# The edge tokens of a neighbour attention move into the first query block, and background work enters between score passes

## Chip, cores and metric

The kernel runs on one core of a Trainium2 chip. The metric is the device time of one execution in microseconds (us). In the text PE is the matrix engine, DVE the vector engine, ACT the scalar engine, POOL the GpSimd engine and SP the engine whose queue issues nearly all DMAs.

## What is computed

Four transformer layers act on one sequence of 2048 tokens with 128 features, all in float32. Each is an attention and a feed-forward part (FFN), both pre-normed and added to the residual `x`:

```
x = x + L0_attn(ln(x)); x = x + L0_ffn(ln(x))   # 16 heads of 8, softmax over all tokens; GELU
x = x + L1_attn(ln(x)); x = x + L1_ffn(ln(x))   # 16 heads of 64, softmax over all 2048 tokens; SiLU gate
x = x + L2_attn(ln(x)); x = x + L2_ffn(ln(x))   # token s sees s-1, s, s+1 (mod 2048); one of 8 experts
x = x + L3_attn(ln(x)); x = x + L3_ffn(ln(x))   # a memory updated in 32 chunks of 64 tokens; 2 of 8 experts + shared
```

Two facts set what may run when. In `L2_attn` each token needs the keys and values of its two neighbours, so a block of 256 tokens needs one token from the block before and one from the block after, and the first token's neighbour is token 2047. In `L3_attn` a state is handed from one chunk of 64 tokens to the next, so the 32 chunks run one after the other.

## The kernel before

**Three parts.** First layer 0 runs with everything it needs. Then the attention of layer 1 runs as a hand-written loop (`l1_attn`, from L1066), the "attention" part below. What follows it for tokens that are ready (layer 1's FFN and all of layers 2 and 3) runs as *background* beside that loop. What background is left when the loop ends is drained in the "tail".

**The attention loop.** `QB` (L33) cuts the 2048 query tokens into five blocks, as (first token, tokens, width). A *unit* is one block and one pair of heads `p`; there are 40 units, eight for each block, and `units` lists them in order. Within a unit the loop of L1136 makes 16 key steps of 128 keys. A step makes four score passes for each of the two heads (the high part of the query `qh` with the high and low parts of the keys `ka`, the low part `ql`, and `mbt` x `onr`, which subtracts a row's maximum), an exp on ACT into `P`, sums of `P` on POOL (`acg`) and DVE (`acd`), and the product of the step before with the values (`P`, `ka`). Between them stand products `km` x `qh` for the maxima of later units, which DVE reduces (`mx`). When a block's eight units are done, `stage_wo` (L1023) applies the output matrix, two pairs at a time, transposes the sum `wac` and adds it to the residual `xs`.

**Edge tokens.** So that layer 2 need not wait for all five blocks, the block (512, 384, 388) carries four more columns: tokens `ex` = 1280, 1792 and 2047, and one of zeros. `u_loadx` (L379) loads them one DMA each; their queries go to `qx`, their maxima through `qx` products of 8 rows (L439). When this block is done, `stage_wo` loads the residual rows of these tokens as `xm` and adds the attention's result. `stage_m` (L1314) carries this small matrix through layer 1's FFN and writes the keys and values of the edges into `edge`. `s_b` (L1959), which starts layer 2's attention of a 256-token block, waits for this `m` and for the blocks that hold neighbours which `ex` does not list.

**Background and order.** The program's order on PE, DVE, ACT and POOL is that in which this Python code emits instructions. Every background stage is a generator, cut into pieces at each `yield`. A `yield 1` asks for a free PSUM bank before the next piece; a `yield "T"` says that the next piece has PE products. `note` (L96) keeps an estimated clock per engine from costs written in L90. `Part.may` (L202) lets a piece in when, by these clocks, its inputs are there and DVE and ACT aren't too far behind. `fill` (L246) takes the first piece that may enter, in the order of `T["order"]`: chunks (`h`), output stages (`d`), then layer 2 and so on, the expert lanes last. With `only="t"` it takes pieces without products alone. The attention loop calls `fill()` twice in each step, after the exps and after the value products. `drain` (L262) empties everything at the end.

**Background stages**, for block `b` of 256 or half-block of 128 tokens: `stage_a` is layer 1's FFN (products `xt` x `wi`), `stage_a2` makes queries, keys and values of layer 2 (`w2m`), `stage_b` its attention (`hb` x `bd8`), `stage_b2` its FFN (`xb`, ending with `oT`); `stage_c` the gates and scans of layer 3's attention, `chunk` (L1626) one state step (`xst` is the new state, `u`, `dz`, `af`, `at` its operands), `stage_d` its output; `stage_g` the router (`rT`), `stage_e0` opens a PSUM bank for the experts of a block, and `s_lane` (L1880) runs the 13 expert tiles of a block, 104 in all, in two lanes and, in the tail, five more. `s_g` lets the router of a block go once the experts of the block before are opened.

Of the kernel before, what the change touches and what calls it, by code (L numbers as in the profile page):

```python
# [14 lines left out]
ALU = mybir.AluOpType  # L15
# [15 lines left out]
ATANH = (1.0000000039388743, 0.3333315796754013, 0.20012426861749952, 0.13980709417165652, 0.14087328632693624)  # L31
T = dict(lead0=22, more0=4, mgap=0.4, pvq=2, lim0=0.5, fq=(3,), pl=-0.5, pr=1.0, tlow=2, tback=3, late=0.3, pvp="mx", mxp="mx", ex=(1280, 1792, 2047), low=1, lows='ge', keep=1, leave=2, pvn=1, sp=0, rdy=40., eu=2, qg=(22, 16, 10), em=2, el=6, sem=0.2, same=1.2, tsame=3.0, order="hdmBbAaEcCeg", ps=dict(st=3, mx=5), dma=2.3, slack=0.1, lim=0.3, backlog=2.5, lead=(10, 8, 6), pp=7, dve=(14, 15), qp=(1, 1), lanes=2, xl=5,
         QB=[(0, 512, 512), (512, 384, 388), (896, 512, 512), (1408, 384, 384), (1792, 256, 256)])  # L33

# [36 lines left out]
def body(ctx: ExitStack, tc: tile.TileContext, x, pa, pb, pc, pi, pd, pr, pr0, pe, pw, out):  # L71
# [122 lines left out]
    class Part:  # L194
# [24 lines left out]
        def step(self):  # L219
            piece[0] = clk["T"]  # L220
            r = next(self.gen, "end")
            self.same = r == "same"
            self.ready = 0.0 if self.same else piece[0] + (r if type(r) is float else 0.0)
            self.pe = r == "T"
            self.banks = r if type(r) is int else 0
            self.seen = len(emitted) if r is False else -1
            if r == "end":
                emitted.add(self.key)
            return r != "end"
# [139 lines left out]
    xnd = dram.tile([128, S], F32, name="xnd")  # L369

    QB = T["QB"]
    EXTRA = T['ex']
    units = [(qb, p) for qb in range(len(QB)) for p in range(NP1)]
    qhh, qfs, kmx, mx1 = {}, {}, {}, {}

    qx = [mid.tile([128, 8], F32R, name=f"qx{i}") for i in range(2)]
    xq = {}

    def u_loadx(qb):  # L379
        t0, tn, n = QB[qb]  # L380
        xq[qb] = l1x.tile([128, 512], F32, name="xq", tag="xq", bufs=2)
        if n != tn:
            ge.memset(xq[qb][:, tn:n], 0.0)
            for i, t in enumerate(EXTRA):
                sy.dma_start(xq[qb][:, tn + i:tn + i + 1], xnd[:, t:t + 1])
        sy.dma_start(xq[qb][:, :tn], xnd[:, t0:t0 + tn])

    def u_qprep(u):
        qb, p = units[u]
        if qb not in xq:  # L390
            u_loadx(qb)
        n = QB[qb][2]
        yield 1
        ps = mi()
        mm(ps[:, :n], C("wq", p * 128, 128), xq[qb][:, :n])
        yield
        qf = l1x.tile([128, 512], F32, name="qf", tag="qf")
        se.activation(qf[:, :n], ps[:, :n], AF.Identity, bias=bq8[:, p:p + 1], scale=0.125)
        rel(ps)
        yield  # L400
        qhh[u] = l1q.tile([128, 512], F32R, name="qh", tag="qh")
        se.copy(qhh[u][:, :n], qf[:, :n])
        yield
        qfs[u] = qf
        tn, n = QB[qb][1:]
        if n > tn:
            for e in range(2):
                r = slice(64 * e, 64 * e + 64)
                se.copy(qx[u % 2][r, 4 * e:4 * e + n - tn], qf[r, tn:n])

# [14 lines left out]
    def u_max(u, i):  # L425

        qb, p = units[u]
        tn, n = QB[qb][1:]
        per = nmax(u) // 4
        c, r = divmod(i, per)  # L430
        qt, e = divmod(r, 2)
        if i == 0:
            mx1[u] = sm.tile([128, 2, 4, 4], F32, name="mx1", tag="mx1")
        if 128 * qt == tn:
            ps = amx()
            mm(ps[0:8], qx[u % 2], kmx[(u, c)])
            ve.tensor_reduce(mx1[u][0:8, 0, 3, c:c + 1], ps[0:8], AX.X, ALU.max)
            rel(ps)
            return 1  # L439
        pss = [amx() for _ in range(2)]  # L440
        for e in range(2):
            rows = slice(64 * e, 64 * e + 64)
            mm(pss[e], qhh[u][rows, qt * 128:(qt + 1) * 128], kmx[(u, c)][rows, :], par=e and 0.02)
        for e in range(2):
            ve.tensor_reduce(mx1[u][:, e, qt, c:c + 1], pss[e], AX.X, ALU.max)
            rel(pss[e])
        return 2

    def u_maxend(u):
# [6 lines left out]
        if n > tn:  # L456
            ve.tensor_reduce(m[0:8, 0, 3:4], mx[0:8, 0, 3, :], AX.X, ALU.max)
        yield 1
        t = mi()
        if n > tn:  # L460
            te.transpose(t[0:1, 256:264], m[0:8, 0, 3:4], ident[0:8, 0:8])
        for e in range(2):
# [4 lines left out]
        if n > tn:  # L467
            for e in range(2):
                se.mul(mbt[u % 2][64 * e:64 * e + 1, tn:n], t[0:1, 256 + 4 * e:256 + 4 * e + n - tn], -1.0)
        rel(t)  # L470
# [552 lines left out]
    def stage_wo(qb, part):  # L1023
# [29 lines left out]
        if n != tn:  # L1053
            ne = len(EXTRA)
            xm = edge_x[0] = sm.tile([ne, 128], F32, name="xm", tag="xm", bufs=1)
            for i, t in enumerate(EXTRA):
                sy.dma_start(xm[i:i + 1, :], xs[t % 128:t % 128 + 1, t // 128, :])
            yield 1
# [7 lines left out]
    def l1_attn():  # L1066
        LEAD = dict(zip((256, 384, 512), T["lead"]))
        LEAD.update({260: LEAD[384], 388: LEAD[512]})
        U = len(units)
# [66 lines left out]
        for g in range(16 * U):  # L1136
# [6 lines left out]
            if u + 2 < U:  # L1143
                if k == 1 and units[u + 2][1] == 0:
                    need(("q", u + 1))
                    u_loadx(units[u + 2][0])
                if k == T["qp"][n <= 256] and u + 2 >= EU:
                    helper(("q", u + 2), u_qprep(u + 2))
# [165 lines left out]
    def stage_m():  # L1314
# [21 lines left out]

        xt = sm.tile([128, 4], F32, name="xtm", tag="xtm", bufs=2)
        yield from norm_T(xt)
        h = sm.tile([128, 12], F32, name="hm", tag="hm", bufs=1)
        for k in range(3):  # L1340
# [3 lines left out]
            yield  # L1344
            th = sm.tile([128, 4], F32, name="thm", tag="thm", bufs=2)
# [3 lines left out]
            ve.scalar_tensor_tensor(h[:, 4 * k:4 * k + ne], th[:, :ne], 0.5, ps[:, 64:64 + ne], ALU.mult, ALU.mult)  # L1349
            rel(ps)  # L1350
            yield 1
        ps = mi()
        for k in range(3):
            mm(ps[:ne, :128], h[:, 4 * k:4 * k + ne], tok(wi, 6 + k), start=(k == 0), stop=(k == 2))
        yield
        ve.tensor_tensor(xm, xm, ps[:ne, :128], ALU.add)
        rel(ps)
        yield
        xt = sm.tile([128, 4], F32, name="xtm", tag="xtm", bufs=2)
        yield from norm_T(xt)  # L1360
        ps = mi()
        for i in range(2):
            mm(ps[:, 4 * i:4 * i + ne], tok(w2m, i), xt[:, :ne])
        yield
        for i in range(2):
            for j, t in enumerate(EXTRA):
                se.activation(edge[:, t // BN, i, int(t % BN > 0):int(t % BN > 0) + 1], ps[:, 4 * i + j:4 * i + j + 1],
                              AF.Identity, bias=b2m[:, i:i + 1])
# [257 lines left out]
    def chunk(b, c):  # L1626
# [48 lines left out]
        ve.scalar_tensor_tensor(u, tht, 2.0, u, ALU.mult, ALU.add)  # L1675
        yield
        mm(da, ef, w2)
# [440 lines left out]
```

## Time and profile before

| what | us |
|---|---|
| median of three runs | 3001.57 (2998.61 to 3004.23) |
| the profiled execution | 3001.08 |
| its span in the profile | 2999.2 |
| PE / DVE / ACT / POOL busy in the span | 2769.9 / 2194.9 / 1582.9 / 1522.3 |
| mean granted PE clock | 0.936 |

The profile's times count from the start of the span. Nearly all instructions are recorded under line L147, since a helper emits them; so groups are told apart by the names of the tiles that they write and read (`mi` is any PSUM bank). A row such as `mi<-km,qh` is a product into PSUM from `km` and `qh`. Matrix products of float32 data show two records each, those of the rounded float32r data one.

### The profile page before, as it was taken

Reading aid. Unit: us, or ns where it says so; the run is one execution under the profiler, and the core shown is the slowest. Engines: PE = TensorE matmul, PEld = TensorE weight load, DVE = VectorE, ACT = ScalarE, POOL = GpSimd, SP = SyncE. Lnnn points to the kernel's source line nnn. Section 1 sums busy time; section 2 is a strip of 40 time slices with the busy share of each in tenths; the row PEclk is TensorE's granted clock in tenths of the full one; section 3 lists DMA queues with packets and bytes.
Section 4 is the critical chain, followed back from the end, with each engine's and each line's share of the span. In section 5 each row is a group of like instructions: output and inputs, shape, how many; then the busy total and the mean of one; then the engine's idle time right before and its main releaser. Section 6 shows DMA issues by size and latency. Waiting matters only on the chain.

```text
span 2999.2 us, 49776 instructions
## 1 busy us (share of the span) xinstructions
PE 2769.9 (92%) x16719; PEld 1307.0 (44%) x16719; DVE 2194.9 (73%) x4699; ACT 1582.9 (53%) x3933; POOL 1522.3 (51%) x1762
## 2 busy tenths in 40 slices
PE   7999999999979899999999999899989898888998
PEld 2222222322234344454444444455544555565666
DVE  7899898898534666566666778887677769787765
ACT  1788887888854444444444444444434334333444
POOL 2400110201127688866776876677767556443444
PEclk9999999999979999999999999999999999776779
DMA  6311231321144333433442332233334343312244
GB/s 142 72 28 22 72 84 17 101 54 46 53 141 135 92 112 110 121 110 111 138 119 87 94 95 87 89 105 108 109 97 114 108 117 94 88 52 61 76 104 115
DMA packets 247749, 275.80 MB, mean 92 GB/s; under 512 B 95747, under 2 KB 183330, under 8 KB 247366
## 3 DMA queue, kind: packets, MB, share of 16 engines
q1 hardware_dynamic: 246630, 272.43, 33.2%
q8 instruction: 132, 2.16, 0.3%
q14 instruction: 123, 1.01, 0.1%
q10 hardware_dynamic: 864, 0.20, 0.0%
HBM read 229.97 MB, written 42.28 MB: 91 GB/s over the span
## 4 chain that ended last, share of the span: by engine, by line
PE 70%; DVE 18%; ACT 6%; issue 3%; DMA 3%; POOL 1%; SPq 0%; ACTq 0%; DVEq 0%; POOLq 0%
PE mi L147 70%; DVE mx L147 5%; ACT P L147 3%; DVE sB L147 1%; DVE o L147 1%; DVE gq L147 1%; DMA ka<-kvd 1%; DVE gt L147 1%; DVE xs L147 1%; ACT kf L147 1%; ACT kh L147 1%; DVE xn L147 1%; DVE sG L147 1%; DVE acd L147 1%; DVE sA L147 0%
## 5 line engine op out<-in xcount | busy, mean ns | idle before, releaser
L147 DVE TENSOR_REDUCE mx<-mi 128x1 f32<-128x512 f32 (+1 forms) x2080 | 1322.1, 683 | 582.8 <-PE mi L147 571.5
L147 ACT ACTIVATE P<-mi 128x512 f32<-128x512 f32 (+3 forms) x2304 | 1137.0, 551 | 1004.1 <-PE mi L147 973.2
L147 POOL TENSOR_TENSOR acg<-acg,P 128x512 f32<-128x512 f32 (+3 forms) x960 | 1011.4, 1083 | 181.8 <-ACT P L147 180.0
L147 PE MATMUL mi<-P,ka 128*64 128x512 f32 (+3 forms) x2560 | 597.6, 546 | 2.3 <-DVE mx L147 2.3
L147 PE MATMUL mi<-qh,ka 64*128 64x512 f32 (+3 forms) x2560 | 521.0, 406 | 9.7 <-DMA ka<-kvd 6.8
L147 PEld LDWEIGHTS mi<-qh,ka 64*128 64x128 f32 x2560 | 247.0, 189 | 382.5 <-issue 347.0
L147 PE MATMUL mi<-kop,qop 48*128 48x512 bf16 x1024 | 348.6, 405 | 24.5 <-DVE mx L147 12.1
L147 PE MATMUL mi<-qop,kop 50*128 50x512 bf16 x1024 | 317.8, 391 | 27.1 <-ACT P L147 24.7
L147 PE MATMUL mi<-P,vop 128*32 128x512 f32 x2048 | 304.3, 623 | 13.9 <-ACT P L147 13.9
L147 POOL TENSOR_SCALAR vep<-mv 128x2 f32<-128x2 f32 (+1 forms) x24 | 5.5, 229 | 495.6 <-DVE mv L147 495.6
L147 PE MATMUL mi<-km,qh 64*128 64x512 f32 x1024 | 225.6, 410 | 30.4 <-DVE mx L147 23.8
L147 PE MATMUL mi<-mbt,onr 64*128 64x512 f32 (+3 forms) x1280 | 228.7, 351 | 1.5 <-DMA mbt<-mb 1.5
L147 PE MATMUL mi<-ql,ka 64*128 64x512 f32 (+3 forms) x1280 | 229.2, 353 | 0.0
L147 PEld LDWEIGHTS mi<-P,ka 128*64 128x64 f32 x2560 | 129.2, 137 | 225.3 <-issue 195.1
L147 PEld LDWEIGHTS <-kop 50*128 50x128 bf16 x1024 | 63.6, 95 | 304.9 <-issue 281.6
L147 POOL TENSOR_TENSOR acg<-P 128x512 f32<-128x512 f32 (+3 forms) x80 | 91.1, 1158 | 202.5 <-DVE acd L147 162.0
L147 PEld LDWEIGHTS mi<-km,qh 64*128 64x128 f32 x1024 | 107.1, 189 | 60.5 <-DVE mx L147 38.5
L147 PEld LDWEIGHTS mi<-mbt,onr 64*128 64x128 f32 x1280 | 124.6, 190 | 13.9 <-DMA mbt<-mb 2.2
L147 PEld LDWEIGHTS mi<-ql,ka 64*128 64x128 f32 x1280 | 125.7, 192 | 0.0
L147 PEld LDWEIGHTS <-qop 48*128 48x128 bf16 x1024 | 72.9, 96 | 97.2 <-issue 82.7
L147 PEld LDWEIGHTS mi<-P,vop 128*32 128x32 f32 x2048 | 55.5, 109 | 119.8 <-issue 90.7
L147 POOL TENSOR_TENSOR kl<-kf,kh 128x512 f32<-128x512 f32 x32 | 40.9, 1278 | 110.9 <-ACT kh L147 82.4
(509 smaller groups left out, 3464.4 us busy)
## 6 DMA issues: line engine op xcount, KB each, us to landing
ka<-kvd SPq DMA_DIRECT2D x320, 384.0 KB
km<-khd SPq DMA_DIRECT2D x159, 256.0 KB
khd<-kh SPq DMA_DIRECT2D x32, 256.0 KB
kvd<-kh SPq DMA_DIRECT2D x32, 256.0 KB
kvd<-kl SPq DMA_DIRECT2D x32, 256.0 KB
kvd<-vt SPq DMA_DIRECT2D x16, 512.0 KB
ka<-in_pw_dram SPq DMA_DIRECT2D x37, 192.0 KB
w3s<-in_pw_dram SPq DMA_DIRECT2D x35, 192.0 KB
```

The source lines that it names most:

```text
L147: r = f(*a, **k)
```

## The change

There are five edits.

1. The blocks become (0, 384, 392), (384, 512, 512) and the three as before. The first block now carries eight more columns: the five edge tokens 256, 768, 1280, 1792 and 2047, and three of zeros. Tiles of the edge row widen from 4 to 8 (`NX`).
2. The order of the units becomes `SEG`: head pairs 0 and 1 of block (384, 512), then all eight pairs of the first block, then pairs 2 to 7 of block (384, 512), then the other blocks.
3. In the attention loop, `fill(9.0, "t")` enters pieces without products after three of the four score passes, after each `fill()` and after each value product. Two pieces that begin with products are now marked so (in `stage_wo` and `chunk`), and a lane's closing piece counts as one too.
4. The loads of `xm` are emitted ahead of the residual add of that block, not behind it, and `wac` has two buffers.
5. Experts of no block are opened before the tail; before, the first block's were.

```
-         QB=[(0, 512, 512), (512, 384, 388), (896, 512, 512), (1408, 384, 384), (1792, 256, 256)])
+T = dict(ti=(0, 1, 2), tf=1, ..., ex=(256, 768, 1280, 1792, 2047), ...
+         QB=[(0, 384, 392), (384, 512, 512), (896, 512, 512), (1408, 384, 384), (1792, 256, 256)])
...
-            self.pe = r == "T"
+            self.pe = r == "T" or type(r) is float
...
-    units = [(qb, p) for qb in range(len(QB)) for p in range(NP1)]
+    SEG = [(1, 0, 2), (0, 0, 8), (1, 2, 8), (2, 0, 8), (3, 0, 8), (4, 0, 8)]
+    units = [(qb, p) for qb, p0, p1 in SEG for p in range(p0, p1)]
+    seg = [i for i, (_, p0, p1) in enumerate(SEG) for _ in range(p0, p1)]
+    NX = 8
...
-            mm(ps[0:8], qx[u % 2], kmx[(u, c)])
-            ve.tensor_reduce(mx1[u][0:8, 0, 3, c:c + 1], ps[0:8], AX.X, ALU.max)
+            mm(ps[0:2 * NX], qx[u % 2], kmx[(u, c)])
+            ve.tensor_reduce(mx1[u][0:2 * NX, 0, 3, c:c + 1], ps[0:2 * NX], AX.X, ALU.max)
...
             mm(ps[:, :n], C("wo", p * 128, 128), O.pop(p)[:, :n], start=(p % 2 == 0), stop=(p % 2 == 1))
-            yield
+            yield "T" if p % 2 == 0 else 0
         if part == 0:
-            w = l1w.tile([128, 512], F32, name="wac", tag="wac", bufs=1)
+            w = l1w.tile([128, 512], F32, name="wac", tag="wac", bufs=2)
...
         del wacc[qb]
+        if n != tn:
+            ne = len(EXTRA)
+            xm = edge_x[0] = sm.tile([ne, 128], F32, name="xm", tag="xm", bufs=1)
+            for i, t in enumerate(EXTRA):
+                sy.dma_start(xm[i:i + 1, :], xs[t % 128:t % 128 + 1, t // 128, :])
+            piece[0] = clk["D"]
         yield 1
...
                     mm(pss[e][:, :n], a[rows], b[rows, :n], start=(i == 0), stop=(i == 3), par=e and 0.02)
+                if T["tf"] and i in T["ti"]:
+                    fill(9.0, "t")
...
             fill()
+            if T["tf"]:
+                fill(9.0, "t")
             if prev:
                 do_sum(*prev[-1])
             if len(prev) == T["pvn"]:
                 while prev:
                     do_pv(*prev.pop(0))
+                    if T["tf"]:
+                        fill(9.0, "t")
                 fill()
+                if T["tf"]:
+                    fill(9.0, "t")
...
         ve.scalar_tensor_tensor(u, tht, 2.0, u, ALU.mult, ALU.add)
-        yield
+        yield "T"
         mm(da, ef, w2)
...
             yield from wait(("g", b))
-            if b and not tail:
-                yield from wait(("l", b - 1))
+            while not tail:
+                yield False
             yield from mark(("e0", b), stage_e0(b))
```

More of the change, by code (lines that the diff above doesn't have):

```diff
@@ L31 @@
 ATANH = (1.0000000039388743, 0.3333315796754013, 0.20012426861749952, 0.13980709417165652, 0.14087328632693624)
-T = dict(lead0=22, more0=4, mgap=0.4, pvq=2, lim0=0.5, fq=(3,), pl=-0.5, pr=1.0, tlow=2, tback=3, late=0.3, pvp="mx", mxp="mx", ex=(1280, 1792, 2047), low=1, lows='ge', keep=1, leave=2, pvn=1, sp=0, rdy=40., eu=2, qg=(22, 16, 10), em=2, el=6, sem=0.2, same=1.2, tsame=3.0, order="hdmBbAaEcCeg", ps=dict(st=3, mx=5), dma=2.3, slack=0.1, lim=0.3, backlog=2.5, lead=(10, 8, 6), pp=7, dve=(14, 15), qp=(1, 1), lanes=2, xl=5,
-         QB=[(0, 512, 512), (512, 384, 388), (896, 512, 512), (1408, 384, 384), (1792, 256, 256)])
+T = dict(ti=(0, 1, 2), tf=1, lead0=22, more0=4, mgap=0.4, pvq=2, lim0=0.5, fq=(3,), pl=-0.5, pr=1.0, tlow=2, tback=3, late=0.3, pvp="mx", mxp="mx", ex=(256, 768, 1280, 1792, 2047), low=1, lows='ge', keep=1, leave=2, pvn=1, sp=0, rdy=40., eu=2, qg=(22, 16, 10), em=2, el=6, sem=0.2, same=1.2, tsame=3.0, order="hdmBbAaEcCeg", ps=dict(st=3, mx=5), dma=2.3, slack=0.1, lim=0.3, backlog=2.5, lead=(10, 8, 6), pp=7, dve=(14, 15), qp=(1, 1), lanes=2, xl=5,
+         QB=[(0, 384, 392), (384, 512, 512), (896, 512, 512), (1408, 384, 384), (1792, 256, 256)])
 def _pack_layout(items):
@@ L372, in body, with u_loadx @@
     EXTRA = T['ex']
-    units = [(qb, p) for qb in range(len(QB)) for p in range(NP1)]
+    SEG = [(1, 0, 2), (0, 0, 8), (1, 2, 8), (2, 0, 8), (3, 0, 8), (4, 0, 8)]
+    units = [(qb, p) for qb, p0, p1 in SEG for p in range(p0, p1)]
+    seg = [i for i, (_, p0, p1) in enumerate(SEG) for _ in range(p0, p1)]
+    NX = 8
     qhh, qfs, kmx, mx1 = {}, {}, {}, {}
-    qx = [mid.tile([128, 8], F32R, name=f"qx{i}") for i in range(2)]
+    qx = [mid.tile([128, 2 * NX], F32R, name=f"qx{i}") for i in range(2)]
     xq = {}
-    def u_loadx(qb):
-        t0, tn, n = QB[qb]
-        xq[qb] = l1x.tile([128, 512], F32, name="xq", tag="xq", bufs=2)
+    def u_loadx(i):
+        t0, tn, n = QB[SEG[i][0]]
+        xq[i] = l1x.tile([128, 512], F32, name="xq", tag="xq", bufs=2)
         if n != tn:
[L383 to L386, printed above, removed]
+            ge.memset(xq[i][:, tn:n], 0.0)
+            for j, t in enumerate(EXTRA):
+                sy.dma_start(xq[i][:, tn + j:tn + j + 1], xnd[:, t:t + 1])
+        sy.dma_start(xq[i][:, :tn], xnd[:, t0:t0 + tn])
     def u_qprep(u):
         qb, p = units[u]
-        if qb not in xq:
-            u_loadx(qb)
+        if seg[u] not in xq:
+            u_loadx(seg[u])
         n = QB[qb][2]
@@ L394, in u_qprep @@
         ps = mi()
-        mm(ps[:, :n], C("wq", p * 128, 128), xq[qb][:, :n])
+        mm(ps[:, :n], C("wq", p * 128, 128), xq[seg[u]][:, :n])
         yield
@@ L408, in u_qprep @@
                 r = slice(64 * e, 64 * e + 64)
-                se.copy(qx[u % 2][r, 4 * e:4 * e + n - tn], qf[r, tn:n])
+                se.copy(qx[u % 2][r, NX * e:NX * e + n - tn], qf[r, tn:n])
     def u_qlow(u):
@@ L456, in u_maxend @@
         if n > tn:
-            ve.tensor_reduce(m[0:8, 0, 3:4], mx[0:8, 0, 3, :], AX.X, ALU.max)
+            ve.tensor_reduce(m[0:2 * NX, 0, 3:4], mx[0:2 * NX, 0, 3, :], AX.X, ALU.max)
         yield 1
@@ L460, in u_maxend @@
         if n > tn:
-            te.transpose(t[0:1, 256:264], m[0:8, 0, 3:4], ident[0:8, 0:8])
+            te.transpose(t[0:1, 256:256 + 2 * NX], m[0:2 * NX, 0, 3:4], ident[0:2 * NX, 0:2 * NX])
         for e in range(2):
@@ L468, in u_maxend @@
             for e in range(2):
-                se.mul(mbt[u % 2][64 * e:64 * e + 1, tn:n], t[0:1, 256 + 4 * e:256 + 4 * e + n - tn], -1.0)
+                se.mul(mbt[u % 2][64 * e:64 * e + 1, tn:n], t[0:1, 256 + NX * e:256 + NX * e + n - tn], -1.0)
         rel(t)
@@ L1053, in stage_wo @@
         if n != tn:
[L1054 to L1057, printed above, removed]
             yield 1
@@ L1067, in l1_attn @@
         LEAD = dict(zip((256, 384, 512), T["lead"]))
-        LEAD.update({260: LEAD[384], 388: LEAD[512]})
+        LEAD[392] = LEAD[512]
         U = len(units)
@@ L1143, in l1_attn @@
             if u + 2 < U:
-                if k == 1 and units[u + 2][1] == 0:
+                if k == 1 and seg[u + 2] > seg[u + 1]:
                     need(("q", u + 1))
-                    u_loadx(units[u + 2][0])
+                    u_loadx(seg[u + 2])
                 if k == T["qp"][n <= 256] and u + 2 >= EU:
@@ L1335, in norm_T @@
             yield 1
-        xt = sm.tile([128, 4], F32, name="xtm", tag="xtm", bufs=2)
+        xt = sm.tile([128, NX], F32, name="xtm", tag="xtm", bufs=2)
         yield from norm_T(xt)
-        h = sm.tile([128, 12], F32, name="hm", tag="hm", bufs=1)
+        h = sm.tile([128, 3 * NX], F32, name="hm", tag="hm", bufs=1)
         for k in range(3):
@@ L1344, in stage_m @@
             yield
-            th = sm.tile([128, 4], F32, name="thm", tag="thm", bufs=2)
+            th = sm.tile([128, NX], F32, name="thm", tag="thm", bufs=2)
             se.activation(th[:, :ne], ps[:, 0:ne], AF.Tanh, scale=0.5)
@@ L1348, in stage_m @@
             ve.scalar_tensor_tensor(th[:, :ne], th[:, :ne], 1.0, ps[:, 0:ne], ALU.add, ALU.mult)
-            ve.scalar_tensor_tensor(h[:, 4 * k:4 * k + ne], th[:, :ne], 0.5, ps[:, 64:64 + ne], ALU.mult, ALU.mult)
+            ve.scalar_tensor_tensor(h[:, NX * k:NX * k + ne], th[:, :ne], 0.5, ps[:, 64:64 + ne], ALU.mult, ALU.mult)
             rel(ps)
@@ L1353, in stage_m @@
         for k in range(3):
-            mm(ps[:ne, :128], h[:, 4 * k:4 * k + ne], tok(wi, 6 + k), start=(k == 0), stop=(k == 2))
+            mm(ps[:ne, :128], h[:, NX * k:NX * k + ne], tok(wi, 6 + k), start=(k == 0), stop=(k == 2))
         yield
@@ L1358, in stage_m @@
         yield
-        xt = sm.tile([128, 4], F32, name="xtm", tag="xtm", bufs=2)
+        xt = sm.tile([128, NX], F32, name="xtm", tag="xtm", bufs=2)
         yield from norm_T(xt)
@@ L1362, in stage_m @@
         for i in range(2):
-            mm(ps[:, 4 * i:4 * i + ne], tok(w2m, i), xt[:, :ne])
+            mm(ps[:, NX * i:NX * i + ne], tok(w2m, i), xt[:, :ne])
         yield
@@ L1366, in stage_m @@
             for j, t in enumerate(EXTRA):
-                se.activation(edge[:, t // BN, i, int(t % BN > 0):int(t % BN > 0) + 1], ps[:, 4 * i + j:4 * i + j + 1],
+                se.activation(edge[:, t // BN, i, int(t % BN > 0):int(t % BN > 0) + 1], ps[:, NX * i + j:NX * i + j + 1],
                               AF.Identity, bias=b2m[:, i:i + 1])
```

## The prediction

> **What bounds the kernel now.** I first read the page's 40 slices (75 us each), where the clock falls in the last seven while PE stays busy, then cut the span at the first and last bias products of layer 1's attention (tile `onr`). Columns: bounds, length, busy time per engine with instruction counts, granted clock, DMA share, GB/s.
>
> ```profile
> PE   7999999999979899999999999899989898888998
> ...
> PEclk9999999999979999999999999999999999776779
> ...
> ```
> ```profile
> L147 PE MATMUL mi<-mbt,onr x1280: 272/335/626, 908.6 to 2593.9; 64*128 64x512 f32 x73, 64*128 64x388 f32 x37, 64*128 64x384 f32 x37, 64*128 64x256 f32 x36
> ...
> ```
> ```profile
> 999.90:1247.50 247.60, 247.60 (x1404) 106.36 (x1402) 151.10 (x238) 121.03 (x229) 201.21 (x157) 1.00 0.36 111
> ```
> ```profile
> 1542.30:2593.90 1051.60, 986.40 (x6328) 504.18 (x6324) 796.69 (x1679) 447.35 (x1284) 716.44 (x815) 0.95 0.36 101
> 2593.90:2999.20 405.30, 345.56 (x1733) 257.12 (x1729) 290.34 (x1074) 160.88 (x662) 167.81 (x280) 0.76 0.31 79
> ```
>
> So there are three parts: layer 0 to 908.6 us, attention of layer 1 for 1685.3 us, and a tail of 405.3 us. Six 512-wide units without background take 247.6 us, 41.3 each, PE without a gap at full clock: there PE is the bound. Once background runs (1542 to 2594), PE idles 65 us of 1052 and DVE is 76% busy. In the tail PE is "busy" 85%, but at clock 0.76, and DVE 72%: no engine is the bound there, a chain is. Its links are visible in the new state of each 64-token chunk, and the expert lanes beside it:
>
> ```profile
> L147 DVE COPY xst<-mi x32: 164/207/217, 1907.8 to 2924.6; 64x64 f32<-64x64 f32 x32
> ...
> ```
> ```profile
> L147 PEld LDWEIGHTS mi<-xe,w3s x140: 119/190/337, 2614.5 to 2979.2; 128*128 128x128 f32 x136, 128*48 128x48 f32 x4
> ...
> ```
>
> 32 chunks must run one after the other, the first ends at 1907.8 and the last at 2924.6. Of these, 14 end by 2594. The other 18 need 330 us, about 17 us each from one copy to the next. Only then come the last expert tiles, to 2999.
>
> How fast the tail is without that chain is seen after the last router product (2951):
>
> ```profile
> 2951.00:2994.00 43.00, 38.67 (x197) 31.19 (x196) 23.57 (x49) 21.98 (x56) 22.11 (x28) 0.92 0.51 109
> ```
>
> Eight matmul records make an expert tile, so 197 records are 24.6 tiles in 43 us: **1.75 us a tile**, at clock 0.92.
>
> **What the change does to the order.** I read it from the two built instruction orders. The edge row, without which no block of layer 2 may start, needed units 0 to 15 before; now it needs units 0 to 9. The first scores of layer 2 move from unit 18 to unit 12, the first chunk from unit 22 to unit 14. With pieces entering between the score passes, chunks stand some 7 key steps apart instead of 9 to 12. Ahead of the last score pass stand 25 chunks instead of 14. After it stand 681 PE products instead of 914; all 104 expert tiles stand after it in both.
>
> **What is added to the attention part.** Score widths sum to 8 x (392+512+512+384+256) instead of 8 x (512+388+512+384+256): 32 more columns of 16416, 0.2%, 3 us at most of some 1430 us that 40 units cost without background. The edge maxima are 32 products in both (16 rows instead of 8: the reduce still reads 512 columns, 683 ns). Two more column loads of the edge tokens, two more `xm` loads and four more key/value writes on ACT (0.28 us each) are beside PE; the column loads now stand on SP near unit 0, where each issue takes 0.3 to 0.6 us ahead of the `ka` loads: bounds 0 to 3 us, taken 0. The pass-on of `xm` loads ahead of the residual add costs nothing: they read rows that layer 0 finished before 890 us.
>
> PE products moved in from the tail, busy time by the rows of 1888 to 2594 us: 11 chunks at 2.0 to 2.5 us (tile `xst` alone covers 27.2 us for 14 chunks; all its kinds summed, 35), about 24; 5 output stages at 2.5, 13; 5 gate-and-scan stages at 3.1, 16; one layer-2 FFN block, 7; less the first router and start of the experts, which go to the tail, 3. Together **56 us**, all on PE, which has no gap there: on the path.
>
> DVE work moved in: 11 chunks at 4 us, 5 gate-and-scan stages at 16, 5 output stages at 3, a router block 6, about 145 us. That is by means of this part, where such rows are stretched:
>
> ```profile
> L147 DVE SCALAR_TENSOR_TENSOR u<-tht,u x32: 169/170/8004, 1888.4 to 2915.4; 64x32 f32<-64x32 f32 x32
> ...
> ```
>
> Units 10 to 39 held 935 us of DVE in 1272; now some 1090 in 1390, 78% instead of 74%. PE's idle share rose from 0 at 61% DVE (999 to 1247) to 6.2% at 76%; along that line 7 to 8% of 1390 is 30 us more than before. The 256-wide units are relieved (fewer DVE pieces stand there than before), and pieces that enter between passes are spread finer. What that is worth no row shows: from -25 (half of what PE now waits for DVE goes) to +60 (the waits double). I take **+24**, a little under the line for the finer spread. Attention: 56 + 24 = **+80**, ends 31 and 116. Where such a piece stands ahead of an exp or a maximum, those queue behind it, and PE for their bank; ACT is 43% busy and covers it, DVE is not, and this is in the 24.
>
> On that stretched row the Trainium skill speaks against the change. "SBUF — State Buffer", section Who interferes with whom, says that a DVE instruction with two inputs in SBUF and a GpSimd instruction that reads SBUF lock each other out for the whole of an instruction. The `u` row (0.17 us at least, 1.14 in the mean before 2594, 0.22 after) agrees in kind, but its 8.0 us is more than one 512-wide GpSimd add of 1.31 us; by the rule alone, an estimate, one such wait per chunk would make 11 x 1.3 = 14 us of DVE, inside the 145.
>
> **What the tail becomes.** The last 256 tokens still start only when attention ends, and their stages stand in the same order. Before, from 2594 the output product's transposes came at 2609, layer 1's FFN to 2651, layer 2's scores at 2667, its FFN's last product at 2725: 131 us with DVE 80% busy (133.4 of 166.1 us from 2593.9 to 2760). The summed DVE work of the tail falls from 322 us by nearly half, so I take 110. Gates and scans 27 (27 to 41 from gate product to scan in this tail; the shortest, with less on DVE); four chunks at 14 (the last ten were 11 to 21 apart, 16 in the mean): 56. That is 193 to the last chunk. Behind it stand 57 of the 104 expert tiles in the built order, 57 x 1.75 = 100. Sum **293** instead of 405: **-112**. Bounds: 255 where PE alone is the limit (104 x 1.75 = 182, plus the other 73 us of PE), and 325 where all goes at the old tail's pace (681 products at 405/914 = 0.44 to 0.48 us).
>
> "TensorE: Matmul & The Clock Gate", What's actually happening, says the clock halves after an idle window of some 3.4 us. The tail's 0.76 against 0.92 in its dense end agrees; by that rule, an estimate, a tail whose PE never idled would turn 345.6 us of busy time at 0.76 into 263.
>
> **Sum.** The profiled run took 3001.08 (span 2999.2, 1.9 around it), 0.5 below the median 3001.57. 3001 + 80 - 112 + 0 = **2969 us**, 1.1% faster. A measurement tells differences above 0.2% (6 us) from no change.
>
> **Rivals.**
> - *The tail becomes PE-bound and the attention absorbs the rest.* For: five blocks' worth of experts is ready when attention ends, seven lanes feed PE, and PE idles 65 us beside background. Against: the last block's chain of 193 us. 3001 + 56 - 150 = 2907. Chance 0.18.
> - *PE stalls at the chunks* (slower). Order is fixed when the program is built; 7 steps of 2.6 us (41.3/16) are 18 us, while chunks in 512-wide units ended 28 to 35 us apart (9 to 12 steps). If a chunk's chain cannot follow, PE waits in order at each of its products, and scores queue behind. It decides from (112 - 56)/25 = 2.2 us per chunk on. At 3.6: 56 + 90 - 112 = +34, 3035. Against: PE now waits only some 4 us in all of 1542 to 2594 for a chunk's operands (`dz`, `kf`, `v2f`, `af`, `at`), and the shorter distance comes from pieces that issue earlier. Chance 0.19.
> - *The gain is given back*: tail 325, since the last block's chain keeps its pace (131 + 36 + 68 + 57 x 1.6), attention +80: 3001. Chance 0.11.
>
> **How the numbers follow.** The forecast has 0.52, itself from 2945 to 2993; the fast rival is all faster, the third about half within 0.2%. Faster 0.52 + 0.18 = 0.70, same 0.08, slower 0.22. The range takes the ends 31 and 116 and the tail's 255 and 325, cut where no more than 2 in 10 is left out: 2905 to 3020.
>
> **What would show it.** Right: last `onr` near 2674 instead of 2594; 25 chunk copies before it; span from there 293 us, with clock above 0.8 and DVE below 65%; the last chunk copy some 190 us after the last score pass, expert tiles for 100 more. Wrong: PE waits for `af`, `dz`, `at`, `xst` that sum to over 55 us in attention (second rival); expert tiles in the tail that wait for a router rather than for PE; or layer 0, which the change does not touch, at another length than 908.6.

## The result, and the profile after

The changed kernel takes **3032.5 us** (median of 4, 3029.8 to 3046.8); the kernel before took 3002.9 beside it. The ratio is 1.0129, 95% interval 1.0084 to 1.0175: 1.3% slower, where 1.1% faster was forecast, and 12 us above the upper end of the range (3020). The profiled execution of after took 3046.8, its span 3045.1. It is the slowest of the four, 14 us over the median, so the parts below add up to somewhat more than the median's loss.

First the page's slices of after (PE's busy tenths and its granted clock, 76 us a slice), then the same cuts as for before: units 2 to 9 (the first block, without background), the attention with background, the tail, and the tail's dense end. Columns as there.

```profile
PE   7998999999979999999899999889999999998788
...
PEclk9999999999979999999989999988999899968888
...
```
```profile
1000.90:1280.00 279.10, 277.00 (x1858) 137.42 (x1858) 178.35 (x303) 137.79 (x324) 212.32 (x208) 1.00 0.42 129
1280.00:2740.20 1460.20, 1356.52 (x8228) 684.60 (x8226) 1121.41 (x2360) 615.17 (x1747) 946.93 (x1047) 0.93 0.32 92
2740.20:3045.10 304.90, 258.14 (x1305) 197.34 (x1303) 207.99 (x680) 132.60 (x445) 142.11 (x210) 0.82 0.43 105
3000.00:3040.00 40.00, 36.72 (x198) 30.07 (x197) 23.96 (x47) 23.39 (x61) 22.80 (x29) 0.96 0.52 119
```

At the end the clock is better: before had five slices of 6 and 7 there, after has four of 8. But between the 20th and the 33rd slice four of 8 appear, where before had 9 throughout, and the 36th, the last of the attention, has a 6. The tail is near what was forecast: 304.9 us instead of 405.3 (forecast 293), at clock 0.82. The attention is not. It ends with the last bias product at 2740 instead of 2594:

```profile
L147 PE MATMUL mi<-mbt,onr x1280: 272/338/792, 907.1 to 2740.2; 64*128 64x512 f32 x74, 64*128 64x384 f32 x37, 64*128 64x392 f32 x36, 64*128 64x256 f32 x36
```
```profile
L147 DVE COPY xst<-mi x32: 204/216/218, 1547.2 to 2929.2; 64x64 f32<-64x64 f32 x32
```

Chunks run from 1547 instead of 1908, and 24 of the 32 have ended by 2740. Cut at the first and last `onr` product, the kernels compare so. "Idle" is the part's length less PE's busy time. "Clock lost" is the time in the part at which PE's clock was granted half, times one half; it is summed from the trace's clock records.

| us | layer 0 | attention | its PE idle | its clock lost | tail |
|---|---|---|---|---|---|
| before | 908.6 | 1685.3 | 78.9 | 58.0 | 405.4 |
| after | 907.1 | 1833.1 | 115.4 | 116.1 | 304.9 |
| difference | -1.5 | +147.8 | +36.5 | +58.1 | -100.5 |

The attention grew by 147.8 us: PE was idle 36.5 longer and busy 111.3 longer (1717.7 instead of 1606.4). Of the busy time 58 go to the halved clock, which leaves 53 for the products moved in (forecast 56). So some 95 us came from waits and from what waits do to the clock, where the forecast had 24.

What PE waited for in after's attention, most first (total us, times, longest):

```profile
PE mi L147 <- DVE mx L147: 41.1, 32, 4.4
PE mi L147 <- DVE dz L147: 22.5, 7, 4.3
PE mi L147 <- DVE m L147: 7.8, 4, 5.4
...
PE mi L147 <- DVE h L147: 4.6, 1, 4.6
```

The same three rows in before:

```profile
PE mi L147 <- DVE mx L147: 36.2, 25, 6.6
PE mi L147 <- DVE m L147: 17.3, 5, 8.9
...
PE mi L147 <- DVE dz L147: 1.4, 2, 0.7
```

So DVE was late, and new is that it was late with a chunk's small operations. One such wait, in order of time (start, length, engine; rows between left out):

```profile
2401.19 7.68 POOL L147 TENSOR_TENSOR acg<-acg,P 128x384 f32<-128x384 f32 x8
...
2403.19 5.72 DVE L147 TENSOR_SCALAR dz<-dzr,rr 64x32 f32<-64x32 f32 x1
...
2404.36 0.33 PE L147 MATMUL mi<-xst,gq 64*64 64x64 f32 x2
...
2408.94 0.22 ACT L147 COPY dz<-dz 64x32 f32<-64x32 f32 x1 [4.34 <-DVE dz L147]
2408.96 0.19 PEld L147 LDWEIGHTS mi<-dz,kcs 64*64 64x64 f32 x2 [4.41 <-DVE dz L147]
2408.97 0.32 PE L147 MATMUL mi<-dz,kcs 64*64 64x32 f32 x2 [4.28 <-DVE dz L147]
```

`dz` is a 64 x 32 operation that takes 0.20 us at its shortest. Here it takes 5.72: it starts while POOL is in a run of eight sums, and ends 0.04 us after the last of them. The product that needs it is next in PE's order, and PE idles 4.3 us. What follows is as costly as the wait (the same place as windows; PE's busy time is the first sum, the granted clock the third number from the end):

```profile
2404.69:2409.11 4.42, 0.14 (x3) 0.15 (x3) 4.42 (x2) 0.17 (x1) 4.18 (x5) 1.00 0.51 167
2409.11:2422.77 13.66, 13.66 (x67) 7.81 (x68) 7.10 (x21) 4.28 (x19) 5.84 (x8) 0.50 0.16 48
2422.77:2436.00 13.23, 12.03 (x98) 7.44 (x96) 10.76 (x39) 5.24 (x21) 4.48 (x7) 1.00 0.34 97
```

A pause of 4.4 us is followed by 13.7 us at half clock, in which PE looks fully busy and makes 67 products where the next 13.2 us make 98. A busy-time column does not show this loss.

All of PE's waits for DVE in the attention come to 97.8 us in after and 67.2 in before. I set beside them what DVE did in those moments, calling "stretched" the part of an instruction beyond 1.3 times the shortest tenth that its form has in any of the runs. DVE was idle in 2 us of them, and never for POOL's results; it was in the stretched part of an instruction for 50 us in after and 27 in before. So it is not late results of POOL that PE and DVE waited for here, and most of the added wait (23 of 31 us) is stretching.

### The profile page after: what moved, and what is told of

Read it like the earlier page. It is cut to its first block, busy times and chain, and to the rows that moved or that the text cites. A ratio compares the mean times of both kernels' runs of the same rounds, so it can differ in the third digit from the quotient of the medians.

```text
span 3045.1 us, 49740 instructions
## 1 busy us (share of the span) xinstructions
PE 2792.0 (92%) x16719; PEld 1312.5 (43%) x16719; DVE 2267.8 (74%) x4700; ACT 1600.2 (53%) x3941; POOL 1524.9 (50%) x1761
## 5 line engine op out<-in xcount | busy, mean ns | idle before, releaser
L147 PE MATMUL mi<-P,ka 128*64 128x512 f32 (+3 forms) x2560 | 616.5, 562 | 0.3 <-DVE dzr L147 0.3
L147 PE MATMUL mi<-qh,ka 64*128 64x512 f32 (+3 forms) x2560 | 533.9, 415 | 9.0 <-DMA ka<-kvd 6.8
L147 PEld LDWEIGHTS mi<-qh,ka 64*128 64x128 f32 x2560 | 254.4, 194 | 383.9 <-issue 347.8
L147 PE MATMUL mi<-km,qh 64*128 64x512 f32 x1024 | 234.2, 416 | 32.6 <-DVE mx L147 25.2
L147 POOL TENSOR_TENSOR acg<-P 128x512 f32<-128x512 f32 (+3 forms) x80 | 96.9, 1230 | 199.7 <-DVE acd L147 122.3
```

What stands on the lines that cost most here:

```text
L147: r = f(*a, **k)
```

## The experiments

Three readings of the trace stood against each other: the chunks stand too close together (the second rival), DVE is overloaded, or POOL's sums hold DVE up. The table gives every run; times are medians, ratios to the runs of before beside them. "Relieved" means that POOL's running sums cover half the columns.

| run | us | ratio (95%) | attention | idle | clock lost | tail |
|---|---|---|---|---|---|---|
| after, no pieces between passes | 3036.8 | 1.0135 (1.0094 to 1.0176) | 1767 | 117 | 91 | 366 |
| pieces between passes alone | 3022.0 | 1.0073 (1.0053 to 1.0093) | 1813 | 116 | 111 | 313 |
| after, chunks spread | 3031.1 | 1.0112 (1.0081 to 1.0143) | 1804 | 120 | 89 | 312 |
| after, planner knows the hold-up | 3037.2 | 1.0129 (1.0108 to 1.0149) | 1830 | 121 | 120 | 300 |
| markers alone | 3010.1 | 1.0031 (1.0014 to 1.0048) | 1714 | 94 | 63 | 377 |
| after, half maxima | 2974.1 | 0.9888 (0.9846 to 0.9930) | 1767 | 91 | 79 | 305 |
| before, half maxima | 2966.4 | 0.9874 (0.9844 to 0.9905) | 1656 | 59 | 53 | 407 |
| after relieved | 2865.8 | 0.9550 (0.9527 to 0.9573) | 1665 | 30 | 36 | 296 |
| before relieved | 2913.1 | 0.9728 (0.9699 to 0.9758) | 1604 | 25 | 29 | 402 |
| pieces alone, relieved | 2891.0 | 0.9635 (0.9599 to 0.9672) | 1674 | 37 | 41 | 304 |
| after relieved, POOL filled up | 2875.7 | 0.9579 (0.9543 to 0.9615) | 1678 | 35 | 44 | 301 |
| after, sums split in two | 3106.5 | 1.0338 (1.0303 to 1.0373) | 1904 | 176 | 140 | 299 |
| after, `dz` on ACT | 3013.9 | 1.0059 (1.0034 to 1.0083) | 1795 | 105 | 89 | 313 |
| before, `dz` on ACT | 3001.0 | 1.0025 (1.0006 to 1.0044) | 1700 | 89 | 70 | 392 |
| pieces alone, `dz` on ACT | 2976.6 | 0.9933 (0.9907 to 0.9958) | 1773 | 97 | 88 | 297 |
| the same, more sums on DVE | 2983.6 | 0.9942 (0.9914 to 0.9970) | 1758 | 92 | 73 | 318 |

**Each part of the change alone.** First the early edges without the pieces, then the pieces without the early edges (`QB`, `ex` and `SEG` as before), then neither, with only the marked pieces, `wac` buffers, `xm` loads and experts' opening.

```
-T = dict(ti=(0, 1, 2), tf=1, ...
+T = dict(ti=(0, 1, 2), tf=0, ...
```

> The changed kernel with its new blocks, but no pieces entered between score passes. 17 chunks stand ahead of the last score pass, 10 to 16 key steps apart, and 842 products behind it (914 before, 681 changed). Theory A (chunks 7 steps apart outrun their own chain; each stalls PE 3 to 4 us beyond its products and drops the clock): the spacing is gone, so attention grows by the moved products alone, 72 x 0.24 = 17 us, tail -32: some 15 us faster than before, 2988. Theory B (every product that moves into attention costs 146/233 = 0.63 us there, whatever the spacing): +45, -32, 3016.

```
...
-ex=(256, 768, 1280, 1792, 2047), ... QB=[(0, 384, 392), (384, 512, 512), ...
+ex=(1280, 1792, 2047), ...           QB=[(0, 512, 512), (512, 384, 388), ...
-    SEG = [(1, 0, 2), (0, 0, 8), (1, 2, 8), (2, 0, 8), (3, 0, 8), (4, 0, 8)]
+    SEG = [(i, 0, 8) for i in range(5)]
...
```

> The changed kernel with the old blocks, old edge tokens and old order of units; pieces do enter between score passes. 23 chunks stand ahead of the last score pass, 6 to 9 steps apart, 702 products behind it. Theory A: 212 x 0.24 = 51 us of products and 23 x 3.6 = 83 us of stalls, tail -95: 3042, as slow as the changed kernel. Theory B: 212 x 0.63 = 133, tail -95: 3041. Theory C (the early edge tokens do the harm): without them the gain remains, 3003 + 51 - 95 = 2959.

The third is the second with `tf=0`:

> The changed code with the old blocks and no pieces between the score passes: what is left of the change is that experts are opened in the tail alone, wac has two buffers, and two pieces are marked. 16 chunks stand ahead of the last score pass, 876 products behind. By 0.63 us for a product that moves in (38) +24, tail -17: 3005, within 0.3% of before. If marks and the held experts cause harm of their own, it is 3020 or more.

Either half alone makes the attention longer by more than it takes off the tail. The markers alone add 9 us by the medians, between their two expectations (their profiled execution, 2998.3, was the fastest of ten, so their row in the table does not show this). In the built order 17, 23 and 16 chunks stand ahead of the last score pass (14 before, 25 after). In the first run they stand 10 to 16 key steps apart, and it is as slow as after: closeness of the chunks is not needed for the loss. Here PE waits for the maxima (63.6 us) and hardly for `dz` (3.1). So no one consumer of DVE is to blame.

**The chunks' distance.** A chunk's first piece is held back by 6 us (`gap=6.0`) of the planner's estimated clock behind the chunk before it:

```
+        if not tail:
+            yield T["gap"]
```

> The changed kernel, but in the attention part a chunk's first piece is held back by 6 us of the planner's clock behind the chunk before it. 22 chunks stand ahead of the last score pass, 9 to 13 steps apart, 727 products behind it. Theory A: 187 x 0.24 = 45 us of products, about 1 us of stall per chunk left, tail -83: 2987, some 45 us faster than the changed kernel. Theory B: 187 x 0.63 = 118, tail -83: 3038, as slow as the changed kernel.

The chunks then stand 9 to 13 steps apart, with 22 ahead of the last score pass. Idle stays at 120 and the time within the noise of after's. The second rival's price was right (146 us over the attention against the 148 measured), but closeness, its mechanism, does not explain the loss.

**A planner that knows the hold-up.** The estimated clock of DVE waits for POOL's where an operation reads two tiles of SBUF:

```
+        if eng == "D" and not in0[0] and sum(len(v.shape) > 1 and math.prod(v.shape[1:]) > 1 and not tname(v).startswith("mi_") for v in ins) > 1:
+            t = max(t, clk["P"])
```

> The changed kernel, with a planner that lets a DVE instruction with two inputs in SBUF start only when its clock of POOL is through; instructions are the same, 24 chunks 6 to 11 steps apart, 688 products behind the last score pass. If the stretched DVE instructions (u, dz, hth) are what the planner lacks, PE's waits for dz go down and the time falls by 15 to 40 us, to 2992 to 3017. Theory A with another cause (piece latency, POOL queue): 3020 to 3035, within 10 us of the changed kernel, as the spacing hardly moves.

Nothing changes, and the run says little. The order hardly moved (only one chunk went to the tail), and the rule passes over `dz`, whose second operand is a single column. Whether an order that goes further could avoid the hold stays open.

**DVE's load, or POOL's hold.** Two cuts at the same order of instructions. Both leave out half of a computation: one of the maxima's reduction, the other of POOL's sums.

```
-            ve.tensor_reduce(mx1[u][:, e, qt, c:c + 1], pss[e], AX.X, ALU.max)
+            nc.vector.tensor_reduce(mx1[u][:, e, qt, c:c + 1], pss[e][:, :256], AX.X, ALU.max)
...
```

> The changed kernel with the same order of instructions, but a query tile's maximum is taken over 256 of each 512 scores (the rest of the maxima is left out, the order is planned as if it were done). It takes some 0.27 us from each of 960 DVE reductions, 260 us of DVE in attention. Theory D (DVE falls behind its planned pace where background is dense, PE waits, and each wait halves the clock for a window): PE idle in attention falls from 115 to some 60, the time lost to half clock from 116 to some 60, attention from 1833 to 1720 us, 2925 to 2945 in all. Theory E (GpSimd's adds hold up DVE and with it the chunks): idle falls by the maxima's own waits alone, 25 us; 3000 to 3020.

> The kernel before with the half maxima of e6, order as before. Under theory D the same relief does less here, since less background stands in attention: idle 79 to 45, lost clock 58 to 35, attention 1685 to 1630, 2945; the two kernels come together or the changed one leads by some 10 us. Under theory E 25 us at most: 2975.

```
-                    eng.tensor_tensor(t[:, :n], t[:, :n], pts[e][:, :n], ALU.add)
+                    h = n if nm == "d" else n // 2
+                    eng.e.tensor_tensor(t[:, :h], t[:, :h], pts[e][:, :h], ALU.add)
...
```

> The changed kernel with the same order, but 24 of 26 sums per unit on GpSimd cover half the columns (the other half of these sums is left out, the order is planned as if it were done). GpSimd's attention work falls by some 400 us. Theory E: stretched u, dz and hth rows go, PE's 22 us of waits for dz and part of the rest go, and their half-clock windows: attention 1833 to 1750 or less, 2950 to 2970. Theory D: DVE's own rows hardly shrink (60 us of stretching out of 1473), attention -20: 3010 to 3025.

> The kernel before, with GpSimd's running sums of P cut to 256 columns (the other half of these sums is left out; VectorE's own sums stay whole, and the order of the instructions is that of before). It is the control for the same cut in the kernel after, which took 167 us off it (2865.8 us). If GpSimd's adds hold up VectorE in general and the change only puts more work under the hold-up, before gains less than after did: attention from 1685 to about 1600, PE's idle time there from 79 to about 35, time 2890 to 2925 us, and after relieved (2866) beats before relieved by 25 to 60 us, which is what the change was forecast to gain. If the hold-up is the same load in both kernels and the loss from the change is its own, before gains as much as after did (about -165, 2835 us), and after relieved stays 30 us slower than before relieved.

Taking some 235 us of work off DVE in the attention gains 58 us in after and 35 in before, each between its two expectations. So DVE's load is a part of the loss: after is now 8 us behind before (2974 against 2966, ranges overlapping) instead of 30. But it does not bring out the forecast gain. Taking 417 us off POOL, with no work taken off DVE or PE, gains 167 in after (2866, where the more hopeful expectation was 2950 to 2970) and 84 in before. DVE's busy time falls with it, by 178 us in after (1341.4 to 1163.2) and 125 in before, though its work is the same: the shorter stretching shown below accounts for nearly all of this. And here the order of the kernels turns, as the first expectation of before relieved had it: **after relieved is 47 us faster than before relieved**. Attention and tail, first of before relieved, then of after relieved:

```profile
906.90:2511.20 1604.30, 1579.17 (x10100) 784.78 (x10102) 1060.45 (x2327) 745.69 (x1925) 783.64 (x1267) 0.98 0.38 112
2511.20:2913.10 401.90, 348.14 (x1733) 259.13 (x1729) 287.57 (x1073) 160.61 (x662) 166.71 (x280) 0.75 0.30 80
```
```profile
907.60:2572.30 1664.70, 1635.07 (x10526) 822.69 (x10528) 1163.15 (x2718) 790.05 (x2150) 812.95 (x1335) 0.98 0.37 108
2572.30:2868.20 295.90, 249.75 (x1307) 192.22 (x1303) 207.78 (x683) 132.86 (x445) 142.09 (x210) 0.86 0.45 108
```

The same move of work, 426 more PE records in the attention, costs 60 us there (PE busy +56, 7 of it by more halved clock, and idle +4.5) and takes 106 off the tail: -46. That is the forecast's sum with hardly any idle term. With whole sums the same move costs 148 in the attention. In the waits of PE in after relieved DVE has nearly vanished:

```profile
PE mi L147 <- DMA ka<-kvd: 8.9, 8, 5.6
PE mi L147 <- DVE mx L147: 5.1, 6, 1.7
...
PE mi L147 <- DVE dz L147: 2.5, 2, 1.5
```

The row `dz` itself, shortest, median and longest in ns, in before, in after and in after relieved:

```profile
L147 DVE TENSOR_SCALAR dz<-dzr,rr x32: 192/233/3676, 1899.7 to 2922.6; 64x32 f32<-64x32 f32 x32
```
```profile
L147 DVE TENSOR_SCALAR dz<-dzr,rr x32: 203/527/5724, 1540.6 to 2927.8; 64x32 f32<-64x32 f32 x32
```
```profile
L147 DVE TENSOR_SCALAR dz<-dzr,rr x32: 192/228/3675, 1505.1 to 2752.7; 64x32 f32<-64x32 f32 x32
```

**How the hold works.** The sums as two instructions of half the columns each; and the relieved kernel with zeros written behind each half sum, so that POOL stays busier:

```
...
+                    if h < n:
+                        eng.e.tensor_tensor(t[:, h:n], t[:, h:n], pts[e][:, h:n], ALU.add)
...
```

> The kernel after, with each of GpSimd's running sums done as two instructions of half the columns (same values, same order). A 512-wide sum took 1.29 us and a 256-wide one 0.75 us, so GpSimd works about 15% longer, near 1420 us of the attention. If VectorE's operation only has to wait for the GpSimd instruction under way, dz and hth get shorter (dz from 1.63 us towards 0.9) and the time falls by 10 to 40 us. If VectorE is kept waiting while GpSimd goes from one instruction to the next, as the 5.7 us of the longest dz suggest, dz stays at 1.6 us or grows and the time goes up by 10 to 60 us.

```
...
+                    if h < n:
+                        ge.e.memset(fl[:, :n - h], 0.0)
...
```

> After relieved (GpSimd's sums cut to 256 columns, the other half of these sums left out), with a write of zeros over 256 columns of a tile that nobody reads behind each of them, so that GpSimd is as busy as in after but reads nothing in that time. If what holds VectorE is GpSimd's reading of two tiles, VectorE's rows stay as short as in after relieved (dz 0.5 us) and the time is 2860 to 2890. If every GpSimd instruction holds VectorE, or if it is GpSimd's own queue that comes late, the time goes back to 2980 to 3040; the rows tell these two apart (dz long again, or short with PE waiting for GpSimd's results).

Split sums cost 74 us more than after, beyond both expectations. The attention of that run:

```profile
905.10:2809.40 1904.30, 1728.64 (x10528) 861.94 (x10528) 1392.79 (x2721) 793.11 (x2150) 1364.80 (x2295) 0.93 0.32 95
```

POOL works 1365 us instead of 1230, and the halves did not let DVE in between: one `hth` (a row of `stage_d`) took 8.4 us, under twelve half sums and a smaller product. The run with zeros must be read with care. POOL got to 1009 us in it, not to after's 1230, and its time (2876) agrees with "only reading holds". But its rows don't: a `dz` took 3.9 us, under four half sums and the zeros between and behind them, and ended as the last zeros did. So writes of zeros hold `dz` too, and the time does not tell the two cases apart. What goes with the stretching is the length of POOL's *runs*. I joined POOL instructions of the attention that follow within 50 ns, and summed how far DVE's instructions exceeded 1.3 times the shortest tenth of their own form:

| | POOL busy | mean run | time in runs over 4 us | DVE stretched by |
|---|---|---|---|---|
| before | 71% | 4.05 us | 791 us | 155 us |
| after | 67% | 3.62 us | 777 us | 239 us |
| before relieved | 49% | 1.45 us | 69 us | 43 us |
| after relieved | 49% | 1.50 us | 94 us | 65 us |
| after relieved, filled up | 60% | 2.06 us | 294 us | 86 us |
| after, sums split | 72% | 5.02 us | 1021 us | 248 us |

Filled up, POOL is 24% busier than relieved (1009 against 813 us), yet its runs stay short, DVE is stretched by 21 us more, and 10 us are lost. In the run with split sums the last column is too small: all eight `o` (a unit's output) of 392 columns were held there (4.5 to 10.4 us each), so even their shortest is stretched. With the shortest tenth that a form has in any of the runs it is 289 us there, against 242 in after and 163 in before. Before has runs as long as after's but stretches less: `dz` by 8 us over 14 chunks instead of 33 over 24, `u` by 13 instead of 23, `hth` by 1 over 6 instead of 24 over 12. There are fewer of these operations, and a `dz` or `hth` was also held less in the mean; why after's order holds each of them longer was not separated. Whether a reader of two tiles holds longer than a writer of zeros stays open.

**The early edges when the hold is gone.** Pieces alone with halved sums:

> Pieces between the passes alone (blocks and edge tokens as before), with GpSimd's sums cut to 256 columns as in the relieved kernels (the other half of these sums is left out). Whole, this order took 3022 us and after 3032. If the early edges cost nothing of their own once the hold-up is gone, it lies within 10 us of after relieved (2866). If they cost something themselves (more small products, one edge path with 8 columns), it is 2835 to 2855; if they gain by themselves, as the forecast had it (11 more products' places for chunks), it is 2877 to 2900.

It takes 2891, 25 us more than after relieved, as the third case had it. So the early edges gain by themselves as forecast, and with the whole sums in place they cost: 10 us on top of the pieces (3032 against 3022, intervals overlapping), and 37 in the pair below (3014 against 2977). Why the sign turns was not separated further. Background then starts six units earlier, beside sums of 512 columns, but that is only argued.

**Ways around it.** The chunk's two worst rows are taken off DVE, in three kernels, and one more key step of sums is moved to DVE in the last.

```
-            se.activation(sq, pv_[0:64, c, 0, :], AF.Square, scale=0.025, accum_out=kk[:, c:c + 1])
+            se.activation(sq, pv_[0:64, c, 0, :], AF.Square, accum_out=kk[:, c:c + 1])
...
-        se.copy(w2, wt)
+        se.mul(w2, wt, 0.025)
...
-        ge.tensor_scalar(u, tht, -1.0, 1.0, ALU.mult, ALU.add)
-        ge.tensor_tensor(u, u, at, ALU.mult)
+        ge.tensor_scalar(u, at, -1.0, 2.0, ALU.mult, ALU.add)
+        ge.tensor_tensor(u, u, tht, ALU.mult)
+        ge.tensor_tensor(u, u, at, ALU.add)
...
-        ve.scalar_tensor_tensor(u, tht, 2.0, u, ALU.mult, ALU.add)
...
-        ve.tensor_scalar(dzn[:, 0, :], dz, rr[:, 3:4], 0.025, ALU.mult, ALU.mult)
+        se.mul(dzn[:, 0, :], dz, rr[:, 3:4])
```

> The kernel after, with the two VectorE operations of a chunk that were held up longest taken off VectorE: dz is scaled by its row factor on ScalarE (the constant 0.025 goes into the copy of w2), and u is computed on GpSimd alone. The result is the same by value. If PE's waits for dz (22.5 us in after's attention against 1.4 in before's) and the halved clock behind them make a good part of the loss, the dz waits fall below 5 us, lost clock falls by 20 to 40 us, and the time is 2975 to 3005 us. If the hold-up is spread over all of VectorE's rows (mx, hth, o, xn), PE waits for the next of them instead and the time stays within 15 us of after's 3032.

> The kernel before with the same edit of a chunk (dz on ScalarE, u on GpSimd alone). PE waits 1.4 us for dz there, so the edit should be worth little: 2990 to 3005 us. If the edit itself is worth something whatever the change (less work on VectorE, 2 operations for each of 31 chunks), before gains as much as after does.

> Background pieces enter between the score passes, the blocks and the four edge tokens stay as before, and a chunk has dz on ScalarE and u on GpSimd alone. Pieces between passes alone took 3022 us, with 16.5 us of PE's waits for dz. If those waits and their halved clock are a good part of the loss: 2970 to 2998 us, faster than both kernels. If the hold-up is spread over all of VectorE's rows: 3008 to 3025 us.

```
-dve=(14, 15)
+dve=(13, 14, 15)
```

> Pieces between the passes, blocks as before, dz on ScalarE and u on GpSimd (2977 us), and one more key step of the 16 of a unit, the 14th, is summed on VectorE instead of GpSimd (3 steps in place of 2). GpSimd loses 80 sums, about 85 us of its 1231 in the attention; VectorE gains 80 adds of some 0.6 us, about 50 us on its 1276. If GpSimd's holding is worth more than VectorE's own time (after relieved lost 413 us of GpSimd and 167 us of time, 0.4 us per us), 85 us give 35 back and 50 us of VectorE cost 50 x 58 / 236 = 12 (half the maxima took 236 us off VectorE and 58 off the time): 2945 to 2965. If VectorE's load decides: 2980 to 3000.

In after the edit gains 19 us, between the two expectations, and the profile says why. PE's waits in that attention:

```profile
PE mi L147 <- DVE mx L147: 32.4, 29, 4.1
PE mi L147 <- DVE e L147: 13.6, 5, 4.1
PE mi L147 <- DMA ka<-kvd: 11.5, 7, 5.3
PE mi L147 <- DVE xst L147: 8.7, 3, 4.0
```

The 22.5 us for `dz` are gone, but `e` went from 4.0 to 13.6, and 8.7 for `xst` are new. Neither of these two is held itself: `e` takes 0.17 us and `xst` 0.22 at most. They stand behind a DVE row that is. This is the longest wait for `xst`, behind an `o` under a run of six sums:

```profile
2007.32 7.42 POOL L147 TENSOR_TENSOR acg<-acg,P 128x512 f32<-128x512 f32 x6
...
2009.04 6.24 DVE L147 TENSOR_TENSOR o<-o,rb 128x512 f32<-128x512 f32 x1
...
2015.21 0.21 DVE L147 COPY xst<-mi 64x64 f32<-64x64 f32 x1
...
2015.47 0.42 PE L147 MATMUL mi<-kf,xst 32*32 32x64 f32 x2 [3.98 <-DVE xst L147]
```

The longest wait for `e` (4.1 us) stands likewise behind an `sB` (a row of `stage_c`) of 5.6 us, and another for `xst` (3.0) behind an `o` of 5.0. In before, where `dz` cost nothing, the edit gains nothing (+4.5 us). With the pieces alone it gains 45 us, and **2976.6 us, ratio 0.9933 (0.9907 to 0.9958), is faster than both kernels**, as its first expectation had it. One more step of sums on DVE makes the attention 15 us shorter and the tail 22 longer, so no gain. The time is that of the expectation by DVE's load, but the attention did get shorter, as the other one had it (by 15 us of 23); why the tail grew was not looked into.

## Why the prediction was wrong, step by step

- *Layer 0, widths, early column loads: nothing.* Held: 907.1 against 908.6, and units 2 to 9 took 34.9 us each (279.1 / 8) with 2 us of PE idle in all and full clock.
- *Products moved in: 56 us.* Held: 53 between before and after (111.3 - 58.1), and 49 between the relieved kernels (55.9 of PE busy time, less 6.8 of halved clock).
- *Moved DVE work: 145 us.* The sum came out (1341.4 - 1185.5 = 156), but by luck: 84 of the 156 are added stretching. Between the relieved kernels the same work is 103 us (1163.2 - 1060.5).
- *Idle in the attention: +24, bounds -25 to +60.* **This step failed.** Idle rose by 36.5, inside the bounds, but the term counted idle alone, and the same term should have held what the pauses cost afterwards. The 58 us of halved clock were not priced at all, though the clock was discussed for the tail. The line "DVE share against PE's idle share" was the wrong view: DVE's share includes the time in which it is held (178 us of 1341 went with half of POOL's sums), and what holds it is POOL's runs.
- *The port rule of the Trainium skill*, "SBUF — State Buffer", Who interferes with whom: the text noted that the 8.0 us row exceeded one sum, and then priced one sum per chunk all the same, 14 us of DVE. The row was right: that `u` of 8.0 us stood under nine sums and a smaller product, and after's holds ran over up to seven sums; DVE was stretched by 84 us more than in before (239 - 155), and relieving POOL is worth 167 us.
- *The tail: -112.* Nearly held, -100.5: 189 us from the last score pass to the last chunk copy instead of 193, then 116 of expert tiles instead of 100. The clock was 0.82 (forecast over 0.8), DVE 208 / 304.9 = 68% (forecast under 65%). The dense end does 198 records in 40 us, 1.62 us a tile instead of 1.75, but that rate did not hold for all of the 116 us.
- *The clock rule* of "TensorE: Matmul & The Clock Gate", What's actually happening: the window shown above agrees, 4.4 us of pause and then half the clock. It belonged in the attention's term as well as in the tail's.
- *The sign given for the second rival*, over 55 us of waits for `af`, `dz`, `at` and `xst`: 22.5 of them are for `dz`, and the rest of that list comes to 2.4. So the sign did not show, though the time came out as this rival had it.

The terms as they should have stood: 53 + 36.5 + 58 - 100.5 - 1.5 = +46 for the profiled pair (measured 3046.8 - 3001.1 = +46).

## What to carry to other kernels

Before moving work beside a stage, look at the stretched rows of the engine that will take it. If an operation's longest time is many times its shortest, the price of one more is the stretched time plus the pause of the engine that waits for it, and here that pause was paid again, and more than once over, in halved clock. Look then at what the holding engine does in that window, and price the *runs* of its instructions, not one of them. Taking single victims off the held engine moves the wait to the next row in its order: here it gained 19 us, halving POOL's sums 167.

## What the runs showed of the hardware that was not expected

- POOL's instructions held DVE's operations for several in a row: in after up to 8.2 us (an `o` of 0.7 us under seven sums), in before up to 10.9 (an `o` under nine). Halving their size without halving their work made it worse (+74 us). Reductions from PSUM (`mx`) were not stretched: 680 or 681 ns in the median and 694 at most in before, in after, and in both relieved kernels.
- A write of zeros on POOL (256 columns, 311 ns) held DVE's `dz` as well:

```profile
L1127 POOL MEMSET fl<- 128x256 f32 x384 | 119.3, 311 | 0.0
```

- In after's attention every stretch of halved clock is a multiple of 3.41 us long (3.41, 6.83, 10.24, 13.65, up to 37.6).
